# Node logits of a graph layer: from TensorE matmuls to VectorE row sums, with a first stage ordered by hand

## The chip, the core and the metric

The kernel runs on one core of a Trainium2 chip. The metric is device time in microseconds (us) of one execution. Times in the profile count from the first instruction of the profiled execution.

Five engines matter. TensorE (PE in the profile, its weight loads PEld) does matmuls and transposes. VectorE (DVE) and ScalarE (ACT) do element-wise work and reductions. GpSimd (POOL) does some more of these. SyncE (SP) issues transfers. ScalarE and GpSimd issue transfers too; `SPq`, `ACTq` and `POOLq` are their instruction queues.

## What is computed

The reference is two graph layers over N = 4096 nodes with 512 features. Each layer normalises its rows, applies relu, and adds an attention output to its input. All is fp32. The change touches the beginning of layer 0:

```python
h = jnp.maximum(_layernorm(x, axis=-1), 0.0)

# layer 0, with h as its input x
node_att = softmax(x @ node_w, axis=0)          # one logit per node
h = x @ edge_w
e = where(adj > 0, h @ h.T, NEG_BIG)
edge_att = softmax(e, axis=1)
support = x @ weight
output = adj * (node_att * edge_att) @ support + bias
```

So from the normalised rows three products are wanted: `x @ edge_w` (512 columns, kept transposed), `x @ weight` (512 columns, called support), and `x @ node_w` (one column, the node logits).

## The kernel before

The program has five stages, one after the other: (1) the three products above, (2) the scores e with row maxima, written to device memory, (3) the attention of layer 0, (4) the projections of layer 1, (5) the attention of layer 1. Stages 3 and 5 are written in an order by hand, inside `tc.manual_schedule()`: there each engine runs its instructions in the order of the program text. In stages 1, 2 and 4 the framework's scheduler picks the order, by the program's dependencies and its own estimates of time. In both cases the framework adds the waits that the data and the buffers ask for. A pool's `bufs` says how many buffers a tile name rotates through; a new tile waits until the last user of its buffer's former content is done. When a pool closes, its memory goes to pools opened later, and their first tiles wait in the same way.

Stage 1 goes over 32 tiles of 128 rows, four tiles to a block of 512 rows, eight blocks. For each tile:

- SP loads the tile `xt` (L119, 256 KB; four buffers).
- `relu_layernorm` (L65 to L77) computes mean and variance on VectorE (L68, L70), the square root on ScalarE (L72), scale and shift on VectorE (L74, L76), and the normalised row with relu on ScalarE (L77, tile `h`, two buffers).
- TensorE transposes four 128 by 128 pieces of `h` into a PSUM bank `pt` (L124), and VectorE copies them into the block's `h_t` (L125).

For each block of four tiles:

- `edge_w` times the transposed block: four column groups `d`, each four calls of 512 columns summed in a bank `pe` (L129), and copied by ScalarE into `he_t` (L131).
- For each tile, `h_t` times `weight`: four calls of 512 columns summed in a bank `ps` (L136), and copied by VectorE into `sup` (L141). Then four calls with one column each give the tile's logits, in column t of the PSUM tile `lg` (L139).

`pt`, `pe` and `ps` have two PSUM banks each; `lg` has one bank of its own. The weights `we` and `ws` (1024 KB each) and `nw` (the 512 node weights as 128 partitions by 4) come on ScalarE's queue in the order `we`, `ws`, `nw`, after the bias (L93, 256 KB).

At the end of stage 1 the logits go through a softmax over all nodes (L145 to L156): maximum on VectorE, across partitions on GpSimd, exp on ScalarE (L151, with its own table load), sum across partitions on GpSimd (L153), reciprocal and multiplication on VectorE (L155, L156).

Stage 2 (L167 to L216) takes `he_t` against itself. SP loads adjacency tiles `ar` and `ac` (L177, L194), TensorE fills a bank `pe`, one of six (L180, four calls per bank, 512 columns or fewer at the diagonal), ScalarE copies the bank to `es` (L183), and VectorE masks it and takes maxima (L186, L187, and L196 to L201).

Of the kernel before, what the change touches and what calls it, by code (L numbers as in the profile page):

```python
# [8 lines left out]
FP = mybir.dt.float32  # L9
AF = mybir.ActivationFunctionType  # L10
ALU = mybir.AluOpType
AX = mybir.AxisListType
PSUM = bass.MemoryType.PSUM
DRAM = bass.MemoryType.DRAM

P = 128
# [12 lines left out]
def kernel(  # L29
# [15 lines left out]
    nc = tc.nc  # L45
    N, F = x.shape
    H, D = 8, 64
    HG = 4
    NT = N // P
    KC = F // P  # L50
    BL = 512
    NB = N // BL
    TB = BL // P
# [3 lines left out]
    ident = const.tile([P, P], FP, name="ident")  # L57
    make_identity(nc, ident)
    eps = const.tile([P, 1], FP, name="eps")
# [5 lines left out]
    def relu_layernorm(h, xt, pool):  # L65

        st = pool.tile([P, 6], FP, name="st")
        nc.vector.bn_stats(st, xt)  # L68
        mv = pool.tile([P, 2], FP, name="mv")
        nc.vector.bn_aggr(mv, st)  # L70
        sd = pool.tile([P, 1], FP, name="sd")
        nc.scalar.activation(sd, mv[:, 1:2], AF.Sqrt, bias=eps)  # L72
        rs = pool.tile([P, 1], FP, name="rs")
        nc.vector.reciprocal(rs, sd)  # L74
        mr = pool.tile([P, 1], FP, name="mr")
        nc.vector.scalar_tensor_tensor(mr, mv[:, 0:1], -1.0, rs, op0=ALU.mult, op1=ALU.mult)  # L76
        nc.scalar.activation(h, xt, AF.Relu, bias=mr, scale=rs)  # L77
# [12 lines left out]
    sup = big.tile([P, NT, F], FP, name="sup")  # L90
# [8 lines left out]
    he_t = hep.tile([P, KC, N], FP, name="he_t")  # L99

    with tc.tile_pool(name="w0", bufs=1) as wp, tc.tile_pool(name="a0", bufs=2) as ap_, tc.tile_pool(
        name="a0s", bufs=4
    ) as sp, tc.tile_pool(name="a0p", bufs=2, space=PSUM) as pp, tc.tile_pool(
        name="a0l", bufs=1, space=PSUM
    ) as lp:
        we = wp.tile([P, KC, F], FP, name="we")
        ws = wp.tile([P, KC, F], FP, name="ws")
        nw = wp.tile([P, KC], FP, name="nw")
        nc.scalar.dma_start(we, edge_w.rearrange("(k p) f -> p k f", p=P))
        nc.scalar.dma_start(ws, weight.rearrange("(k p) f -> p k f", p=P))  # L110
        nc.scalar.dma_start(nw, node_w)
        lg = lp.tile([P, NT], FP, name="lg")

        for b in range(NB):
            h_t = ap_.tile([P, KC, BL], FP, name="h_t")
            for j in range(TB):
                t = b * TB + j
                xt = sp.tile([P, F], FP, name="xt")
                nc.sync.dma_start(xt, x[t * P:(t + 1) * P, :])  # L119
                h = sp.tile([P, F], FP, name="h", bufs=2)  # L120
                relu_layernorm(h, xt, sp)
                pt = pp.tile([P, KC, P], FP, name="pt")
                for k in range(KC):
                    nc.tensor.transpose(pt[:, k, :], h[:, k * P:(k + 1) * P], ident)  # L124
                nc.vector.tensor_copy(h_t[:, :, j * P:(j + 1) * P], pt)  # L125
            for d in range(KC):
                pe = pp.tile([P, BL], FP, name="pe")
                for k in range(KC):
                    nc.tensor.matmul(pe, we[:, k, d * P:(d + 1) * P], h_t[:, k, :],  # L129
                                     start=(k == 0), stop=(k == KC - 1))  # L130
                nc.scalar.copy(he_t[:, d, b * BL:(b + 1) * BL], pe)  # L131
            for j in range(TB):
                t = b * TB + j
                ps = pp.tile([P, F], FP, name="ps")
                for k in range(KC):
                    nc.tensor.matmul(ps, h_t[:, k, j * P:(j + 1) * P], ws[:, k, :],  # L136
                                     start=(k == 0), stop=(k == KC - 1))
                for k in range(KC):
                    nc.tensor.matmul(lg[:, t:t + 1], h_t[:, k, j * P:(j + 1) * P], nw[:, k:k + 1],  # L139
                                     start=(k == 0), stop=(k == KC - 1))  # L140
                nc.vector.tensor_copy(sup[:, t, :], ps)  # L141


        m1 = sp.tile([P, 1], FP, name="m1")
        nc.vector.tensor_reduce(m1, lg, AX.X, ALU.max)  # L145
        m2 = sp.tile([P, 1], FP, name="m2")
        nc.gpsimd.partition_all_reduce(m2, m1, P, bass_isa.ReduceOp.max)
        m3 = sp.tile([P, 1], FP, name="m3")
        nc.vector.tensor_scalar(m3, m2, -1.0, None, ALU.mult)
        s1 = sp.tile([P, 1], FP, name="s1")  # L150
        nc.scalar.activation(na, lg, AF.Exp, bias=m3, accum_out=s1)  # L151
        s2 = sp.tile([P, 1], FP, name="s2")
        nc.gpsimd.partition_all_reduce(s2, s1, P, bass_isa.ReduceOp.add)  # L153
        s3 = sp.tile([P, 1], FP, name="s3")
        nc.vector.reciprocal(s3, s2)  # L155
        nc.vector.tensor_scalar(na, na, s3, None, ALU.mult)  # L156


    with tc.tile_pool(name="mx", bufs=1) as mxp, tc.tile_pool(name="b_a", bufs=6) as adjp, tc.tile_pool(
        name="b_e", bufs=4  # L160
    ) as esp, tc.tile_pool(name="b_m", bufs=2) as mkp, tc.tile_pool(name="b_s", bufs=2) as sp, tc.tile_pool(
        name="b_p", bufs=6, space=PSUM
# [5 lines left out]
        for i in range(NB):  # L168
            for j in range(i, NB):
                for t in range(i * TB, (i + 1) * TB):  # L170
# [7 lines left out]
                    pe = p_e.tile([P, BL], FP, name="pe")  # L178
                    for k in range(KC):
                        nc.tensor.matmul(pe[:, :w], he_t[:, k, rows], he_t[:, k, cols],  # L180
                                         start=(k == 0), stop=(k == KC - 1))
# [24 lines left out]
            for j in range(TB):  # L206
                t = i * TB + j
# [12 lines left out]
    with tc.tile_pool(name="c_e", bufs=9) as etp, tc.tile_pool(name="c_b", bufs=4) as ebp, tc.tile_pool(  # L220
        name="c_a", bufs=12
    ) as adjp, tc.tile_pool(name="c_w", bufs=3) as wkp, tc.tile_pool(name="c_t", bufs=3) as atp, tc.tile_pool(
        name="c_m", bufs=2
    ) as mxp, tc.tile_pool(name="c_o", bufs=4) as iop, tc.tile_pool(name="c_s", bufs=2) as sp, tc.tile_pool(
        name="c_p", bufs=1, space=PSUM
    ) as p_o, tc.tile_pool(name="c_q", bufs=3, space=PSUM) as p_t, tc.tile_pool(
        name="c_r", bufs=1, space=PSUM
# [34 lines left out]
        def turn(b, m):  # L262

            i = m % TB
            n = TB if m // TB > b else i if m // TB == b else 0
            eb = src[b, m]
            parts = []
            if n > 0:
                pt = p_t.tile([P, BL], FP, name="pt")
                for j in range(n):  # L270
                    nc.tensor.transpose(pt[:, j * P:(j + 1) * P], eb[:, j, i * P:(i + 1) * P], ident)  # L271
                parts.append((slice(0, n * P), pt))
            if n < TB:
                parts.append((slice(n * P, BL), eb[:, i, :] if m // TB == b else eb))
            src[b, m] = parts
# [77 lines left out]
    with tc.tile_pool(name="w1", bufs=1) as wp, tc.tile_pool(name="a1", bufs=3) as sp, tc.tile_pool(  # L353
        name="a1p", bufs=3, space=PSUM
# [15 lines left out]
        for t in range(NT):  # L370
            xt = sp.tile([P, F], FP, name="xt", bufs=4)
            nc.sync.dma_start(xt, x1[t * P:(t + 1) * P, :])
            h = sp.tile([P, F], FP, name="h")
            relu_layernorm(h, xt, sp)
            pt = pp.tile([P, KC, P], FP, name="pt")
            for k in range(KC):
                nc.tensor.transpose(pt[:, k, :], h[:, k * P:(k + 1) * P], ident)
            h_t = sp.tile([P, KC, P], FP, name="h_t")
# [56 lines left out]
    with tc.tile_pool(name="e", bufs=3) as ep, tc.tile_pool(name="e3", bufs=2) as e3p, tc.tile_pool(  # L435
        name="z", bufs=6
    ) as zp, tc.tile_pool(name="rl", bufs=2) as rlp, tc.tile_pool(name="p", bufs=2) as prp, tc.tile_pool(
        name="ac", bufs=2
    ) as acp, tc.tile_pool(name="io1", bufs=2) as iop, tc.tile_pool(name="os", bufs=1) as osp, tc.tile_pool(
        name="s1", bufs=1  # L440
    ) as sp, tc.tile_pool(name="p_v", bufs=1, space=PSUM) as p_v, tc.tile_pool(
        name="p_x", bufs=1, space=PSUM
# [184 lines left out]
```

## Time and profile before

| | us |
|---|---|
| median of 3 runs | 3289.96 (3289.59 to 3289.97) |
| profiled execution | 3290.54 |
| its span, first to last instruction | 3288.7 |
| TensorE busy in the span | 3117.9 (95%) |
| VectorE busy | 2573.5 (78%) |
| ScalarE busy | 1195.6 (36%) |
| GpSimd busy | 1415.7 (43%) |
| last logit matmul of stage 1 starts | about 283.4 |
| first matmul of stage 2 starts | 283.75 |
| last matmul of stage 2 starts | 741.2 |

In the profile a line `L139` is line 139 of the kernel. A group line reads: line, engine, operation, output<-inputs, shapes, count | busy us, mean ns of one | idle time of the engine just ahead of them and what ended it. A chain line reads: start, length in us, what set the time there. A line of busy time by stretch reads: stretch, its length, then busy us and count for TensorE, its weight loads, VectorE, ScalarE and GpSimd, then the granted TensorE clock, the share of DMA, and GB/s. A fp32 matmul call shows as two matmul records, a transpose as one. A matmul's own duration overlaps with its neighbours', so the pace of TensorE is read from starts.

### The profile page before, as it was taken

Reading aid. Unit: us, or ns where it says so; the run is one execution under the profiler, and the core shown is the slowest. Engines: PE = TensorE matmul, PEld = TensorE weight load, DVE = VectorE, ACT = ScalarE, POOL = GpSimd, SP = SyncE. Lnnn points to the kernel's source line nnn. Section 1 sums busy time; section 2 is a strip of 40 time slices with the busy share of each in tenths; the row PEclk is TensorE's granted clock in tenths of the full one; section 3 lists DMA queues with packets and bytes.
Section 4 is the critical chain, followed back from the end, with each engine's and each line's share of the span. In section 5 each row is a group of like instructions: output and inputs, shape, how many; then the busy total and the mean of one; then the engine's idle time right before and its main releaser. Section 6 shows DMA issues by size and latency. Waiting matters only on the chain.

```text
span 3288.7 us, 34545 instructions
## 1 busy us (share of the span) xinstructions
PE 3117.9 (95%) x11514; PEld 1291.8 (39%) x11514; DVE 2573.5 (78%) x3593; ACT 1195.6 (36%) x1417; POOL 1415.7 (43%) x1081
## 2 busy tenths in 40 slices
PE   8999999998999999999998869999999999999997
PEld 4554444444444444444444423232323232323332
DVE  3324777776667678788896599898989898999997
ACT  2211111111111111111113256565656666666664
POOL 0001111113434445445454546565656565655554
PEclk9999999998999999999999989999999999999999
DMA  2104666656444444454433179898988898989896
GB/s 74 39 20 158 225 219 229 223 182 211 142 141 155 142 157 159 141 163 157 147 107 103 36 188 223 228 218 225 219 224 217 222 223 224 222 227 219 227 221 161
DMA packets 239250, 577.07 MB, mean 175 GB/s; under 512 B 26048, under 2 KB 51936, under 8 KB 239072
## 3 DMA queue, kind: packets, MB, share of 16 engines
q1 hardware_dynamic: 163680, 357.76, 32.7%
q0 software_dynamic: 55680, 196.13, 26.9%
q10 hardware_dynamic: 19712, 20.98, 2.1%
q8 instruction: 90, 1.47, 0.2%
q14 instruction: 88, 0.72, 0.1%
HBM read 389.02 MB, written 51.53 MB: 134 GB/s over the span
## 4 chain that ended last, share of the span: by engine, by line
PE 62%; DVE 18%; issue 6%; ACT 6%; DMA 4%; POOL 2%; ACTq 0%; DVEq 0%; SPq 0%; POOLq 0%
PE po L324 26%; PE pe L180 14%; DVE pr L489 13%; PE pv L516 8%; ACT e L474 5%; PE ps L136 3%; PE pe L129 3%; PE dn L522 2%; DMA z<-z_d 2%; PE pd L382 2%; PE pt L271 2%; DMA y<-x 1%; POOL pr L387 1%; PE lg L139 1%; DVE d L283 1%
## 5 line engine op out<-in xcount | busy, mean ns | idle before, releaser
L516 PE MATMUL pv<-pr,va 128*64 128x512 f32 x4096 | 1025.2, 610 | 61.5 <-DVE pr L489 40.2
L324 PE MATMUL po<-sup,at 128*128 128x512 f32 x2048 | 915.2, 598 | 45.1 <-DVE at L291 45.1
L498 POOL TENSOR_TENSOR acc<-acc,pr 128x1024 f32<-128x1024 f32 x240 | 570.3, 2376 | 434.2 <-DVE pr L489 434.0
L489 DVE SCALAR_TENSOR_TENSOR pr<-z,g_m,ex 128x1024 f32<-128x1024 f32 x512 | 631.4, 1273 | 41.9 <-DMA z<-z_d 41.9
L516 PEld LDWEIGHTS pv<-pr,va 128*64 128x64 f32 x4096 | 359.4, 137 | 686.0 <-issue 378.7
L324 PEld LDWEIGHTS po<-sup,at 128*128 128x128 f32 x2048 | 380.2, 192 | 479.7 <-issue 403.7
L301 POOL TENSOR_TENSOR racc<-racc,ex 128x512 f32<-128x512 f32 x240 | 354.7, 1478 | 467.4 <-ACT ex L285 466.8
L285 ACT ACTIVATE ex<-d 128x512 f32<-128x512 f32 x256 | 161.3, 630 | 829.0 <-DVE d L283 829.0
L180 PE MATMUL pe<-he_t 128*128 128x512 f32 (+3 forms) x1152 | 455.8, 557 | 0.1
L465 ACT ACTIVATE ex<-e 128x1024 f32<-128x1024 f32 x256 | 263.1, 1028 | 456.6 <-DVE pr L489 356.9
L486 DVE SCALAR_TENSOR_TENSOR pr<-rl,gd_m,ex 128x1024 f32<-128x1024 f32 x256 | 326.0, 1274 | 29.1 <-ACT ex L465 29.1
L489 DVE SCALAR_TENSOR_TENSOR pr<-z,g_m,e 128x1024 f32<-128x1024 f32 x256 | 327.6, 1280 | 0.0
L477 ACT ACTIVATE rl<-z,ngd_m,d_m 128x1024 f32<-128x1024 f32 x256 | 314.1, 1227 | 26.9 <-DMA z<-z_d 26.9
L180 PEld LDWEIGHTS pe<-he_t 128*128 128x128 f32 x1152 | 212.9, 190 | 234.5 <-issue 222.5
L474 ACT ACTIVATE e<-e,ld_m 128x1024 f32<-128x1024 f32 x256 | 290.0, 1133 | 5.0 <-DMA z_d<-zs 5.0
L283 DVE TENSOR_TENSOR d<-d,mk 128x512 f32<-128x512 f32 x256 | 273.7, 1069 | 8.8
L522 PE MATMUL dn<-pr,d_m 128*32 128x512 f32 x2048 | 273.8, 607 | 0.0
L184 POOL DMA_DIRECT2D e_d<-es x144 | 79.2, 550 | 351.3 <-ACT es L183 345.8
L282 DVE TENSOR_TENSOR d<-pt,mb 128x512 f32<-128x512 f32 (+2 forms) x136 | 87.4, 643 | 172.6 <-PE pt L271 172.6
L183 ACT COPY es<-pe 128x512 f32<-128x512 f32 (+2 forms) x144 | 79.3, 551 | 376.2 <-PE pe L180 376.2
L504 POOL DMA_DIRECT2D acc<-pr x240 | 208.2, 868 | 5.0 <-DVE pr L486 4.0
L291 DVE TENSOR_TENSOR at<-ex,a 128x512 f32<-128x512 f32 x256 | 190.5, 744 | 0.5
(116 smaller groups left out, 2182.9 us busy)
## 6 DMA issues: line engine op xcount, KB each, us to landing
e<-in_adj_t_dram SPq DMA_DIRECT2D x256, 512.0 KB, 4.5
acc<-pr POOLq DMA_DIRECT2D x256, 512.0 KB, 4.9
a<-in_adj_t_dram SPq DMA_DIRECT2D x256, 256.0 KB, 3.4
ar<-in_adj_dram SPq DMA_DIRECT2D x120, 256.0 KB, 3.1
e_d<-es POOLq DMA_DIRECT2D x120, 256.0 KB, 2.8
ac<-in_adj_t_dram SPq DMA_DIRECT2D x112, 256.0 KB, 3.2
eb<-e_d SPq DMA_DIRECT2D x28, 1024.0 KB, 5.8
et<-e_d SPq DMA_DIRECT2D x112, 256.0 KB, 3.5
```

The lines of the kernel that those rows point to most:

```text
L180: nc.tensor.matmul(pe[:, :w], he_t[:, k, rows], he_t[:, k, cols], start=(k == 0), stop=(k == KC - 1))
L283: nc.vector.tensor_tensor(d, d, mk, ALU.add)
L301: nc.gpsimd.tensor_tensor(racc, racc, e, ALU.add)
L324: nc.tensor.matmul(po[j], w[:, j * P:(j + 1) * P], sup[:, m, :], start=(m == 0), stop=last)
L465: nc.scalar.activation(x_, ra.pop((i, m)), AF.Exp)
L474: nc.scalar.activation(x_, ra[i, m], AF.Exp, bias=ld_m[:, h + 3, m:m + 1])
L477: nc.scalar.activation(r, zs_[i, 0], AF.Relu, bias=ngd_m[:, h, m:m + 1], scale=d_m[:, h, m:m + 1])
L486: nc.vector.scalar_tensor_tensor(w, rl.pop((i, m)), gd_m[:, h, m:m + 1], x_, op0=ALU.add, op1=ALU.mult)
L489: nc.vector.scalar_tensor_tensor(w, zs_[i, k], g_m[:, h + k, m:m + 1], e3.pop((i, m)) if k == 3 else x_, op0=ALU.max, op1=ALU.mult)
L498: nc.gpsimd.tensor_tensor(acc[i, 3], acc[i, 3], w, ALU.add)
L516: nc.tensor.matmul(v[c][q][r * D:(r + 1) * D, :], va[:, m, g * HG + k, :], pr[i, m, k][:, q * BL:(q + 1) * BL], **flags)
L522: nc.tensor.matmul(dn[r * Q:(r + 1) * Q, :], d.to_broadcast([P, Q]), pr[i, m, k][:, q * BL:(q + 1) * BL], **flags)
```

## The change

Five things change, all in stage 1.

- The logits are no longer matmuls. For each tile VectorE multiplies `h` by the node weights and sums along the row, in one `tensor_tensor_reduce`, into column t of `lg`, which is now an SBUF tile.
- For that, each partition needs all 512 node weights. `nw` is spread by four small matmuls: column k, repeated 128 times, against the identity puts weights 128k to 128k+127 into every row of `pw`. One VectorE copy takes them to `nw_b`.
- `nw` is loaded first on SP's queue; on ScalarE's queue `ws` now comes ahead of `we`, two transfers as before.
- The stage is in an order by hand. Tiles 0 to 3 are normed one by one, with the support of a tile after the transposes of the next. From then on, a block's four groups of edge products alternate with the transposes of the next block's four tiles, while the tile three ahead is normed; the next block's four supports follow.
- `xt` and the small tiles have eight buffers, `h` five.

The softmax at the end is as it was, inside the order by hand, and stage 2 is unchanged.

```diff
-        name="a0s", bufs=4
-    ) as sp, tc.tile_pool(name="a0p", bufs=2, space=PSUM) as pp, tc.tile_pool(
-        name="a0l", bufs=1, space=PSUM
-    ) as lp:
+        name="a0s", bufs=8
+    ) as sp, tc.tile_pool(name="a0p", bufs=2, space=PSUM) as pp, tc.manual_schedule():
...
+        nw_b = wp.tile([P, F], FP, name="nw_b")
         nw = wp.tile([P, KC], FP, name="nw")
+        nc.sync.dma_start(nw, node_w)
+        nc.scalar.dma_start(ws, weight.rearrange("(k p) f -> p k f", p=P))
         nc.scalar.dma_start(we, edge_w.rearrange("(k p) f -> p k f", p=P))
-        nc.scalar.dma_start(ws, weight.rearrange("(k p) f -> p k f", p=P))
-        nc.scalar.dma_start(nw, node_w)
-        lg = lp.tile([P, NT], FP, name="lg")
-
+
+        pw = pp.tile([P, KC, P], FP, name="pt")
+        for k in range(KC):
+            nc.tensor.matmul(pw[:, k, :], nw[:, k:k + 1].to_broadcast([P, P]), ident, start=True, stop=True)
+        nc.vector.tensor_copy(nw_b.rearrange("p (k q) -> p k q", k=KC), pw)
+        lg = wp.tile([P, NT], FP, name="lg")
+        xts, mvs, sds, hs, hts = {}, {}, {}, {}, {}
+
+        def fetch(t):
+            xts[t] = sp.tile([P, F], FP, name="xt")
+            nc.sync.dma_start(xts[t], x[t * P:(t + 1) * P, :])
+
+        def stats(t):
+            st = sp.tile([P, 6], FP, name="st")
+            nc.vector.bn_stats(st, xts[t])
+            mvs[t] = sp.tile([P, 2], FP, name="mv")
+            nc.vector.bn_aggr(mvs[t], st)
+            sds[t] = sp.tile([P, 1], FP, name="sd")
+            nc.scalar.activation(sds[t], mvs[t][:, 1:2], AF.Sqrt, bias=eps)
+
+        def norm(t):
+            rs = sp.tile([P, 1], FP, name="rs")
+            nc.vector.reciprocal(rs, sds.pop(t))
+            mr = sp.tile([P, 1], FP, name="mr")
+            nc.vector.scalar_tensor_tensor(mr, mvs.pop(t)[:, 0:1], -1.0, rs, op0=ALU.mult, op1=ALU.mult)
+            hs[t] = sp.tile([P, F], FP, name="h", bufs=5)
+            nc.scalar.activation(hs[t], xts.pop(t), AF.Relu, bias=mr, scale=rs)
+
+        def turn(t):
+            b, j = divmod(t, TB)
+            if j == 0:
+                hts[b] = ap_.tile([P, KC, BL], FP, name="h_t")
+            h = hs.pop(t)
+            pt = pp.tile([P, KC, P], FP, name="pt")
+            for k in range(KC):
+                nc.tensor.transpose(pt[:, k, :], h[:, k * P:(k + 1) * P], ident)
+            hw = sp.tile([P, F], FP, name="hw", bufs=2)
+            nc.vector.tensor_tensor_reduce(hw, h, nw_b, 1.0, 0.0, ALU.mult, ALU.add, lg[:, t:t + 1])
+            nc.vector.tensor_copy(hts[b][:, :, j * P:(j + 1) * P], pt)
+
+        def support(t):
+            b, j = divmod(t, TB)
+            ps = pp.tile([P, F], FP, name="ps")
+            for k in range(KC):
+                nc.tensor.matmul(ps, hts[b][:, k, j * P:(j + 1) * P], ws[:, k, :],
+                                 start=(k == 0), stop=(k == KC - 1))
+            nc.vector.tensor_copy(sup[:, t, :], ps)
+
+        def edges(b, d):
+            pe = pp.tile([P, BL], FP, name="pe")
+            for k in range(KC):
+                nc.tensor.matmul(pe, we[:, k, d * P:(d + 1) * P], hts[b][:, k, :],
+                                 start=(k == 0), stop=(k == KC - 1))
+            nc.scalar.copy(he_t[:, d, b * BL:(b + 1) * BL], pe)
+
+        done = {fetch: 0, stats: 0, norm: 0}
+
+        def upto(f, t):
+            while done[f] < min(t + 1, NT):
+                f(done[f])
+                done[f] += 1
+
+        def step(t):
+            if t < NT:
+                ahead = 0 if t < TB else 3
+                for u in range(t, t + ahead + 1):
+                    upto(fetch, u + 4)
+                    upto(stats, u)
+                    upto(norm, u)
+                    upto(stats, u + 1)
+                turn(t)
+
+        for t in range(TB):
+            step(t)
+            if t > 0:
+                support(t - 1)
+        support(TB - 1)
         for b in range(NB):
-            h_t = ap_.tile([P, KC, BL], FP, name="h_t")
             for j in range(TB):
...
+                edges(b, j)
+                step((b + 1) * TB + j)
+            if b + 1 < NB:
+                for j in range(TB):
+                    support((b + 1) * TB + j)
```

What is left out of the diff is the body of the former loop, removed: L117 to L141 as printed above.

More of the change, by code (lines that the diff above doesn't have):

```diff
@@ L114 @@
+        support(TB - 1)
         for b in range(NB):
-            h_t = ap_.tile([P, KC, BL], FP, name="h_t")
             for j in range(TB):
[L117 to L141, printed above, removed]
+                edges(b, j)
```

## The prediction

> **What bounds the kernel now.** I read the page's chain of waits first. It gives TensorE 62% of the span and names three lines of the first stage:
>
> ```profile
> PE 62%; DVE 18%; issue 6%; ACT 6%; DMA 4%; POOL 2%; ACTq 0%; DVEq 0%; SPq 0%; POOLq 0%
> PE po L324 26%; PE pe L180 14%; DVE pr L489 13%; PE pv L516 8%; ACT e L474 5%; PE ps L136 3%; PE pe L129 3%; PE dn L522 2%; DMA z<-z_d 2%; PE pd L382 2%; PE pt L271 2%; DMA y<-x 1%; POOL pr L387 1%; PE lg L139 1%; DVE d L283 1%
> ```
>
> Then I read the same chain in order of time over one block of four tiles (start, length, what), here from 66.18 to 85.92 us:
>
> ```profile
> 66.18 1.72 PE ps L136 x4
> 67.89 0.79 PE lg L139 x8
> 68.68 3.54 PE ps L136 x8
> 72.22 0.79 PE lg L139 x8
> ...
> 80.87 0.79 PE lg L139 x8
> 81.66 0.51 PE pt L124 x4
> 82.25 0.82 ACT h L77
> 83.11 0.66 PE pt L124 x4
> ...
> 85.92 13.92 PE pe L129 x32
> ```
>
> The same piece repeats every 33.67 us (the `ACT h` pieces start at 48.58, 82.25, 115.91, ...). Everything in it is TensorE's, but for one wait for h. Logits (L139) stand on the path, 0.79 us a tile. The last one of the stage is at 282.88, and the second stage's L180 starts at 283.75.
>
> Third, busy time by stretch (TensorE, its loads, VectorE, ScalarE, GpSimd, then clock and DMA): one stretch in the first stage and one in the second.
>
> ```profile
> 100.00:150.00 50.00, 49.41 (x180) 26.74 (x178) 12.47 (x29) 7.34 (x14) 0.00 (x0) 1.00 0.07 21
> 300.00:400.00 100.00, 100.00 (x250) 46.01 (x249) 75.06 (x184) 17.10 (x31) 17.50 (x32) 1.00 0.72 245
> ```
>
> VectorE has 75% free in the first, so it can take work over. The second is TensorE's too: L180 holds the chain without a gap from 283.75 to 741. A start of stage two that is earlier by x ends it earlier by x.
>
> Last, the groups, for durations:
>
> ```profile
> L139 PE MATMUL lg<-nw,h_t 128*128 128x1 f32 x256 | 30.3, 240 | 0.0
> L187 DVE CUSTOM_DVE_ANT_0 mk<-pe,mk 128x512 f32<-128x512 f32 x14 | 9.7, 690 | 9.2 <-ACT es L183 9.0 <-DVE mk L186 0.2
> L187 DVE DVE_READ_ACCUMULATOR2_ANT rm<- 128x1 f32 x17 | 1.4, 83 | 0.0
> ```
>
> L139 has 256 records for 128 calls, two for each fp32 product, as L129 and L136 have. L187 is the same VectorE call that the change uses for row sums.
>
> [...]
>
> **The steady block.** 32 of the 64 wide matmuls take 13.84 us (L129 starts at 52.18, the next line at 66.02), so one takes 0.4287 us with 0.12 for the switch. A group of four transposes takes 0.43 to 0.51.
> - Removed: four logits of 0.81 us (67.73 to 68.54 by start times) = 3.24 us, and the 0.52 us wait for h at 83.1.
> - What is left is 33.67 - 3.76 = 29.91. From below: 64 x 0.4287 + 4 x 0.48 + 0.3 for switches = 29.7. I take 29.8.
> - VectorE per tile: statistics 0.69 + 0.18, scale and shift 0.15 + 0.15, row sum 0.69 + 0.08, two copies 1.38: 3.3 us of a tile's 7.45. ScalarE: 0.29 + 0.81 + 0.58 = 1.7. Both lie beside TensorE.
> - Lead of three: in `step(t)` tile t+3 is normed and t is turned. h(t+3) is queued on ScalarE behind the copy of `edges(b, j)`, so it comes about 1.6 us after that matmul group ends (0.2 + 0.58 + 0.81), and is wanted three steps (3 x 3.9 us) later. `pt`, `pe` and `ps` have two banks each, and each copy is due a step after it can run. So I cost waits in the steady blocks at nothing; the cover is some 10 us, and without it a step pays the 1.6.
> - SP's fetches have eight buffers: x(t+4) goes into one freed four tiles before; DMA is 7% busy here.
>
> **The start.** Here the lead is nought, and VectorE's order puts the copy of `support(t-1)` ahead of the scale of tile t+1.
> - `nw` now goes first on SP. Its issue took 0.88 us on ScalarE's queue, so x slips from 6.2 to about 7.1. The eight small matmuls (about 1.1, as eight transposes took 1.07) and the copy to `nw_b` (0.69) stand ahead of all VectorE work. If `nw` lands by 5 (bias, asked for at 0.72, took 5.7 with 256 KB), `nw_b` is ready at 7.2. If x0 and `nw_b` are ready at 6.4, or `nw_b` only at 9.2, all moves by -0.8 or +2.
> - Statistics from 7.2, h(0) at 9.7, `turn(0)`; then row sum, copy, scale, h(1) at 12.4, `turn(1)`; `support(0)` from 12.95. `ws` is now the first of the two weights, and the first landed at 11.0 (L109); `we` is wanted only at 31.9. So the order of transfers costs nothing.
> - `support(0)` ends at 16.4. Then 0.2 + 0.69 (copy) + 0.3 (scale, shift) + 0.81 (h) = 2.05 us with TensorE idle, before `turn(2)`; the same before `turn(3)`. Four supports of 3.43, two turns of 0.5 and two gaps: 31.9.
> - `edges(0,0)` to 35.3, then 1.6 us idle for h(4), behind its ScalarE copy; `turn(4)` from 36.9. Tiles 4 to 7 are normed in that step in one row, some 1.75 us each, with the row sum and copy of tile 4 behind them on VectorE (43.6). The first that needs its bank is `turn(6)`, at 44.75: 1.1 us to spare. Three more edges, four turns, four supports: 62.9.
>
> **The sum.** 62.9 + 6 blocks x 29.8 + the last four edges 13.7 = 255.4 us, where L180 can start; before it was 283.7. The gain is 28.3 us. Against before, logits give 32 x 0.81 = 25.9 and the waits for h some 4; the start gives back about 2.
>
> **Into the second stage.** Its first adjacency load is issued at 287.46, just after the last softmax step at 287.15 (L156), 3.7 us after TensorE changed over. After, maximum and sum over `lg` run while the last edges do, but the exp is queued on ScalarE behind the last `he_t` copy: 0.8 + 1.28 + 0.29 + 0.19, then GpSimd 0.39 and VectorE 0.16 + 0.24 with hand-overs, again about 3.7. TensorE fills six `pe` buffers meanwhile: (512+384+256+128)/512 + 2 = 4.5 groups of 3.43 = 15.4 us. The first came free at 293.26 (end of L198), 9.6 after the change. So 5.8 us of further delay is hidden; beyond that every us counts.
>
> The profiled execution has 3290.54 us for a span of 3288.7; 3262.2 after the sum. The median shown is 3289.96, hence 3261.7.
>
> **Rivals.**
> 1. *The lead covers only part* (chance 0.14). Say every second block boundary or turn pays: 14 of 28 steps x 1.0 us = 14, to about 3276 (3268 to 3284). Also under this: the second stage, planned by itself, comes out in a worse order and spoils its gapless 457 us. For it: the memset of L167 ran among the softmax steps, so the two stages had been ordered together. Against it: VectorE is at 75% there and TensorE needs no luck.
> 2. *The gain is swallowed* (0.02): loads of the second stage start late enough to stop TensorE. That takes 5.8 + 28.3 = 34 us of delay, and 3290 results. Nothing in the page is that late.
> 3. *Slower* (0.04): the order by hand makes TensorE wait at every step, because the lead isn't real (tile t's h is tied to the copy just before it). Then each of the 28 steps costs the startup's 1.6 to 2.05 us: 45 to 57, less 28.3: 3307 to 3319. It decides from 28.3 / 28 = 1.0 us a step on. Against it: h has five buffers, four of them live.
> That the row sum isn't off TensorE can't be: no matmul writes `lg` any more.
>
> **How the numbers follow.** My forecast, with 0.80, is 3256 to 3268: start +2 or -0.8, a block 0.3 lower to 0.7 higher over six (-2 to +4). A floor is 235.5 us of pure TensorE work (512 x 0.4287 + 32 x 0.5) from 9.7 on, 245, thus 3252. To hold 8 in 10 with part of rival 1, the range is 3255 to 3271. About 0.2% (6.6 us) is what a measurement of this kernel can tell from no change. Forecast and rival 1 lie below it: 0.94 faster; 0.02 within; 0.04 slower.
>
> **What would show it.** L180's first matmul at 255 (252 to 264). Blocks 29.8 us apart. Two idle gaps of 2 us for h ahead of the third and fourth group of transposes, one of 1.6 ahead of the fifth, and none later. Row sums of 690 + 83 ns, 32 of each. First adjacency load 3 to 5 us after L180 starts, and no wait at L180. Wrong, if TensorE waits for h or for a copy past 50 us, or if the span from L180's start to the end isn't 3005 us within 3.

## The result

The changed kernel takes 3261.2 us, median of 4 runs (3256.1 to 3263.1), against 3289.8 us for the kernel before in the same rounds. The ratio is 0.9915, with a 95% interval of 0.9897 to 0.9932: 0.85% faster. The forecast was 3261.7 us. The profiled execution has 3259.88 us and a span of 3258.1. Lines have moved: L180 of before, the first matmul of stage 2, is now L235; the edge products are L162, the supports L155, the transposes L146, h L137, the row sum L148.

The page's chain of waits, after. The logits are gone from it; the edge products and supports are still there with 3% each:

```profile
PE 61%; DVE 19%; issue 6%; ACT 6%; DMA 4%; POOL 2%; ACTq 0%; DVEq 0%; POOLq 0%; SPq 0%
PE po L379 26%; PE pe L235 14%; DVE pr L544 14%; PE pv L571 8%; ACT e L529 5%; PE pe L162 3%; PE ps L155 3%; DMA z<-z_d 2%; PE dn L577 2%; PE pd L437 2%; PE pt L326 2%; POOL pr L442 1%; DMA y<-x 1%; ACT ex L520 1%; DVE d L338 1%
```

The same chain in order of time (start, length, what), one block and the end of the stage:

```profile
95.52 3.43 PE pe L162 x8
98.95 0.44 PE pt L146 x4
99.39 3.43 PE pe L162 x8
...
110.57 0.44 PE pt L146 x4
111.00 13.74 PE ps L155 x32
124.74 3.43 PE pe L162 x8
...
241.63 13.75 PE pe L162 x32
255.38 0.02 issue
255.40 0.59 ACT he_t L164
...
256.04 44.09 PE pe L235 x114
```

A block now takes 124.74 - 95.52 = 29.22 us; it took 33.67. Nothing in it belongs to another engine. At the end there is a wait that was nearly hidden before: stage 2's first matmul starts 0.66 us after the last edge products, behind ScalarE's copy of them.

TensorE's instructions in order of time at the start of the stage (start, length, line, shapes, idle before and what ended it):

```profile
10.87 1.12 PE L146 MATMUL pt<-ident,h 128*128 128x128 f32 x4 [3.16 <-ACT h L137]
13.88 1.11 PE L146 MATMUL pt<-ident,h 128*128 128x128 f32 x4 [1.89 <-ACT h L137]
14.79 5.27 PE L155 MATMUL ps<-ws,h_t 128*128 128x512 f32 x8
21.95 0.66 PE L146 MATMUL pt<-ident,h 128*128 128x128 f32 x4 [1.89 <-ACT h L137]
...
27.94 0.66 PE L146 MATMUL pt<-ident,h 128*128 128x128 f32 x4 [1.89 <-ACT h L137]
...
35.30 3.60 PE L162 MATMUL pe<-h_t,we 128*128 128x512 f32 x8
40.28 0.66 PE L146 MATMUL pt<-ident,h 128*128 128x128 f32 x4 [1.39 <-ACT h L137]
```

The three idle gaps ahead of the third, fourth and fifth group of transposes are the forecast ones. A full group of eight wide matmuls reads 3.60 here, as its last end is modelled; by the pace, 3.43 a group, the gaps are 0.17 us longer than the brackets say. The first support (14.79) reads 5.27, and that was not forecast.

The groups of the first stage and its busy time in one stretch (TensorE, loads, VectorE, ScalarE, GpSimd, clock, DMA share, GB/s):

```profile
L148 DVE CUSTOM_DVE_ANT_0 hw<-h,nw_b 128x512 f32<-128x512 f32 x32 | 21.3, 665 | 0.2
L148 DVE DVE_READ_ACCUMULATOR2_ANT lg<- 128x1 f32 x32 | 2.6, 83 | 0.0
```

```profile
100.00:150.00 50.00, 50.00 (x139) 23.50 (x138) 20.85 (x56) 10.83 (x23) 0.00 (x0) 1.00 0.15 43
```

The row sums cost VectorE 24 us in all (665 + 83 ns each; 690 + 83 were forecast), and it still has more than half of the stretch free; TensorE has none.

Stage 2 now starts at 256.04 in place of 283.75, which is 27.7 us earlier. Its matmuls take 457.5 us as before (457.4). The rest of the profiled gain is in the stages behind that, and no part of the change: from the start of stage 2 to the end of the span it is 3004.9 us before and 3002.1 after, while the twelve profiled executions of this study have 2997.7 to 3007.4 there with the same code. So the measure below is where stage 2 starts; the time is given beside it.

### The profile page after: what moved, and what is told of

It is laid out like the page before. It is cut to its first block, busy times and chain, and to the rows that moved or that the text cites. A ratio compares the mean times of both kernels' runs of the same rounds, so it can differ in the third digit from the quotient of the medians.

```text
span 3258.1 us, 34087 instructions
## 1 busy us (share of the span) xinstructions
PE 3092.7 (95%) x11266; PEld 1265.4 (39%) x11266; DVE 2598.7 (80%) x3658; ACT 1193.0 (37%) x1417; POOL 1415.1 (43%) x1081
## 4 chain that ended last, share of the span: by engine, by line
PE 61%; DVE 19%; issue 6%; ACT 6%; DMA 4%; POOL 2%; ACTq 0%; DVEq 0%; POOLq 0%; SPq 0%
PE po L379 26%; PE pe L235 14%; DVE pr L544 14%; PE pv L571 8%; ACT e L529 5%; PE pe L162 3%; PE ps L155 3%; DMA z<-z_d 2%; PE dn L577 2%; PE pd L437 2%; PE pt L326 2%; POOL pr L442 1%; DMA y<-x 1%; ACT ex L520 1%; DVE d L338 1%
## 5 line engine op out<-in xcount | busy, mean ns | idle before, releaser
L235 PE MATMUL pe<-he_t 128*128 128x512 f32 (+3 forms) x1152 | 455.8, 557 | 0.7 <-ACT he_t L164 0.7
L235 PEld LDWEIGHTS pe<-he_t 128*128 128x128 f32 x1152 | 212.9, 190 | 235.8 <-issue 222.5
## 6 DMA issues: line engine op xcount, KB each, us to landing
a<-in_adj_t_dram SPq DMA_DIRECT2D x256, 256.0 KB, 3.1
ar<-in_adj_dram SPq DMA_DIRECT2D x120, 256.0 KB, 2.9
e_d<-es POOLq DMA_DIRECT2D x120, 256.0 KB, 2.7
ac<-in_adj_t_dram SPq DMA_DIRECT2D x112, 256.0 KB, 3.1
et<-e_d SPq DMA_DIRECT2D x112, 256.0 KB, 3.2
```

## The experiments

Each kernel was profiled once, the changed kernel twice. Its two profiles differ by 1.4 us in where stage 2 starts, all of it from the start of stage 1; so a difference of that size between two kernels means nothing by itself. Each ratio is to runs of the kernel before in the same rounds, so it differs a little from the quotient of the medians shown.

The theory: the removed logit matmuls are nearly the whole gain, since they stood on the path that sets the end, and the order by hand adds little because its start gives back what its steady part wins. The first rival: the order is the gain. The second: the lead of three tiles is what keeps the order from being slower than before.

| kernel | stage 2 starts (us) | median (us) | ratio to before (95%) |
|---|---|---|---|
| before | 283.75 | 3289.8 | |
| changed | 256.0 | 3261.2 | 0.9915 (0.9897 to 0.9932) |
| order alone | 281.6 | 3288.3 | 0.9994 (0.9987 to 1.0) |
| row sums alone | 257.7 | 3262.9 | 0.9912 (0.9896 to 0.9929) |
| lead 0 | 298.8 | 3304.0 | 1.0038 (1.0023 to 1.0053) |
| lead 1 | 258.1 | 3260.1 | 0.9907 (0.9892 to 0.9921) |
| start with lead 1 | 249.6 | 3255.1 | 0.9895 (0.9879 to 0.9912) |
| start: lead, pace, later copy | 247.7 | 3253.0 | 0.9885 (0.9872 to 0.9899) |
| changed, again | 257.5 | 3261.6 | 0.9914 (0.99 to 0.9927) |

**The order alone.** The logits go back to TensorE:

```diff
-            nc.vector.tensor_tensor_reduce(hw, h, nw_b, 1.0, 0.0, ALU.mult, ALU.add, lg[:, t:t + 1])
...
+            for k in range(KC):
+                nc.tensor.matmul(lg[:, t:t + 1], hts[b][:, k, j * P:(j + 1) * P], nw[:, k:k + 1],
+                                 start=(k == 0), stop=(k == KC - 1))
             nc.vector.tensor_copy(sup[:, t, :], ps)
```

> The order by hand with the logits as matmuls again (four one-column calls behind each tile's support, lg in PSUM; no spreading of the node weights, no row sums). Theory (the removed logit matmuls are nearly the whole gain, and the order itself wins only the waits for h, less what its start gives back): the first stage ends at 256.0 + 32 x 0.81 = 281.9 us, 281 to 283 with a start that no longer waits for the spread weights; the time is 3286 to 3290. Rival (the order is the gain, and the row sums only ride on it): the stage ends before 272, the time is below 3280.

Measured: stage 2 starts at 281.6, 2.1 us earlier than before. In time that can't be told from nothing: 0.9994, with 1.0 at the edge of the interval. The rival wanted less than 272. The chain of this run over one block:

```profile
70.31 3.54 PE pe L159 x8
...
89.34 0.79 PE lg L152 x8
90.12 3.54 PE ps L149 x8
93.67 0.78 PE lg L152 x8
...
103.11 3.54 PE pe L159 x8
```

A block takes 32.80 us, 0.87 less than before and 3.58 more than in the changed kernel. From one group of logits to the next it is 4.33 us (89.34 to 93.67), and eight support matmuls alone take 3.43. So a tile's logits cost 0.90 us here, and not the 0.81 from their own start to the next: the support behind them takes 3.54.

**The row sums alone.** The kernel before, its order by the scheduler kept:

```diff
+        pw = pp.tile([P, KC, P], FP, name="pt")
+        for k in range(KC):
+            nc.tensor.matmul(pw[:, k, :], nw[:, k:k + 1].to_broadcast([P, P]), ident, start=True, stop=True)
+        nc.vector.tensor_copy(nw_b.rearrange("p (k q) -> p k q", k=KC), pw)
...
                 nc.vector.tensor_copy(h_t[:, :, j * P:(j + 1) * P], pt)
+                nc.vector.tensor_tensor_reduce(hw, h, nw_b, 1.0, 0.0, ALU.mult, ALU.add, lg[:, t:t + 1])
...
-                for k in range(KC):
-                    nc.tensor.matmul(lg[:, t:t + 1], h_t[:, k, j * P:(j + 1) * P], nw[:, k:k + 1],
-                                     start=(k == 0), stop=(k == KC - 1))
```

> The kernel before with the row sums alone: order by the scheduler as before, four xt buffers, the node weights first on SP and spread by the four small matmuls, we before ws. Theory: 283.75 - 32 x 0.81 = 257.8 us for the first stage; the waits for h of the old order stay, and a row sum of 0.77 us may stand ahead of a copy of transposed pieces once or twice per block, which adds nothing to 12: 258 to 270, the likeliest 260, the time 3263 to 3276. Rival (the order is the gain): the stage ends after 275, the time is above 3280.

Measured: 257.7, which is 26.05 us earlier than before, against 32 x 0.81 = 25.9. The time is the changed kernel's within its scatter. The chain of this run still has the wait for h once in each block; its last three lines are the change of stage:

```profile
47.28 0.82 ACT h L77
48.10 0.13 issue
48.23 0.63 PE pt L127 x4
...
65.61 11.16 PE ps L141 x26
...
77.29 0.82 ACT h L77
...
256.86 0.69 DVE sup L143
257.55 0.15 DVE acc L169
257.70 12.30 PE pe L182 x40
```

So its block takes 30.01 us (77.29 less 47.28), 3.66 less than before: four times the 0.90 that a tile's logits cost in the order by hand, too. That 26.05 is so near to 25.9 is therefore partly luck. From the first edge products to stage 2 it is 236.0 us here (from 21.70) and 264.3 before (from 19.47), 28.3 less; of that the later start takes 2.2. In the chain of the start an x tile lands at 12.76 (10.77 before), and the copy of the node weights and two row sums follow; what made the tile late was not tested.

The order by hand takes 0.8 us out of each block, 5.5 over seven, yet ends only 1.7 us earlier (0.2 by the second profile of the changed kernel). The wait at the change of stage is no longer there than in this run, so its start gives the rest back, some 4 us. In the steady blocks no row sum came in ahead of a needed copy in a way that shows, so that part of the expectation was too cautious; in the start two did, and TensorE waited 0.36 us for the copy behind them. Alone, the two parts give 2.1 + 26.05 = 28.2 us, together 27.7: within the scatter of the start they add up. The first rival is out.

**A lead of nought and of one.**

```diff
-                ahead = 0 if t < TB else 3
+                ahead = 0
```

```diff
-                ahead = 0 if t < TB else 3
+                ahead = 0 if t < TB else 1
```

> The changed kernel with a lead of nought everywhere: each tile is normed in the step that turns it. Theory: each of the 28 steps of the steady part pays what the first one paid in the changed kernel, 1.54 us (hand-over, copy of he_t on ScalarE, h): 27 more x 1.54 = 42, the first stage ends at 298, the time is 3303. Rival (the lead does nothing, since ScalarE is mostly idle): 256 and 3261.

> The changed kernel with a lead of one tile in place of three. Theory: h of the next tile is ready some 1.6 us after a group of edge products ends and is wanted 3.9 us after that, so a lead of one hides it all: the first stage ends at 256 (within 0.5), the time is that of the changed kernel. Rival (three are needed, since ScalarE's and VectorE's queues couple the tiles): the stage ends after 265.

With a lead of nought, every step of the steady part has the gap (TensorE in order of time):

```profile
75.27 0.66 PE L146 MATMUL pt<-ident,h 128*128 128x128 f32 x4 [1.39 <-ACT h L137]
75.77 3.60 PE L162 MATMUL pe<-h_t,we 128*128 128x512 f32 x8
80.75 0.66 PE L146 MATMUL pt<-ident,h 128*128 128x128 f32 x4 [1.39 <-ACT h L137]
```

A step takes 80.75 - 75.27 = 5.48 us in place of 3.87, so 1.61 more. Stage 2 starts at 298.8, and the kernel is slower than before, 3304.0 us: the prediction's third rival, with its mechanism and nearly its price (it said 3307 to 3319). With a lead of one the gap is gone. Stage 2 starts at 258.1, outside the 0.5 that was expected, but from the first edge products on (37.38 against 35.30) the two are alike: 220.7 us to the start of stage 2 in both. The 2.1 us are the start's, where the second support ran slow as well. So one tile of lead hides what three hide.

**The start with a lead of one.** This is for the gaps, and for a version that beats the changed kernel:

```diff
-                ahead = 0 if t < TB else 3
+                ahead = 1 if t < TB else 3
```

> The changed kernel with a lead of one tile in the start too (tiles 0 to 3), three afterwards as before. Theory (the three idle gaps of the start come from the scale of a tile being queued on VectorE behind the copy of a support, and from h(4) being queued on ScalarE behind a copy of he_t): both gaps of 2.05 us and the one of 1.54 go, the first stage ends 5.6 us earlier, at 250.4, or 248 to 253 with the scatter of the first landings; the time is about 3255. Rival (the gaps are x tiles that come late): they stay, 256.

Measured: 249.6 and 3255.1. After the first support TensorE has no gap up to stage 2, so all three came from the queues and none from late x tiles.

**The slow first support.** In the changed kernel the eight matmuls of the first support take some 5.1 us, not 3.43; the first four start 0.85 us apart, the others 0.43. Two causes were at hand: transfers into the same memory, which go on until about 17 us, or TensorE itself after a pause. This run fills pauses with matmuls that nobody reads:

```diff
+        dm = pp.tile([P, BL], FP, name="pe")
+
+        def warm(n):
+            for _ in range(n):
+                nc.tensor.matmul(dm[:, :P], ident, ident, start=True, stop=True)
+
+        warm(8)
         pw = pp.tile([P, KC, P], FP, name="pt")
...
+        warm(6)
         for t in range(TB):
             step(t)
+            if t == 0:
+                warm(6)
```

> The changed kernel with idle TensorE time at the start filled: 8 + 6 + 6 matmuls of the identity with itself into a bank that nobody reads, before and after the matmuls that spread the node weights and after the first transposes. Theory (TensorE runs at half pace after having been idle, and that stretched the first support from 3.43 to 5.1 us and the spreading to 2.04): the first support takes 3.4 to 3.9 us, the first stage ends 1 to 2.5 us earlier. Rival (the first support is slow because transfers of x and the weights write into the same memory until about 18 us): it still takes about 5, from the same start.

TensorE in order of time, this run; L162 is here the support:

```profile
14.10 3.60 PE L162 MATMUL ps<-ws,h_t 128*128 128x512 f32 x8
19.60 0.66 PE L153 MATMUL pt<-ident,h 128*128 128x128 f32 x4 [1.90 <-ACT h L144]
20.09 5.29 PE L162 MATMUL ps<-ws,h_t 128*128 128x512 f32 x8
```

The first support is at full pace, at about the same time (14.10 against 14.79) and under no fewer transfers: in the four us from 14 DMA moved 387, 381, 238 and 98 GB/s in this run, and 387, 383, 207 and 121 in the changed kernel. So transfers are not the cause. But the stage ended later (stage 2 from 257.1): the half pace came back in the second support, and again in the third, each behind a gap of 1.9 us. The granted clock of the second says so too. Busy time over the second support of this run (the seventh figure is the granted clock, the eighth the share of DMA):

```profile
20.10:24.00 3.90, 3.90 (x8) 1.71 (x7) 0.87 (x3) 0.00 (x0) 0.00 (x0) 0.60 0.22 67
```

Transfers had fallen to 22% by then. So the half pace goes with TensorE's pauses, though not every pause brings it: in the changed kernel the second support follows a gap of 1.89 us and runs at full pace. That filling some pauses gains time by itself was wrong, as long as others follow. (One run, 3264.1 us.)

**All of it together.** Lead of one in the start, the pauses filled, and the copy of the node weights moved from its old place to behind the scale of tile 0 (the other edits are those above, with five matmuls in place of six after the first transposes):

```diff
                     upto(norm, u)
+                    if t == 0 and u == 0:
+                        nc.vector.tensor_copy(nw_b.rearrange("p (k q) -> p k q", k=KC), pw)
```

> The changed kernel with three edits of the start together: a lead of one tile for tiles 0 to 3 (ended the first stage at 249.6 alone), matmuls of the identity with itself in TensorE's idle time there (8 + 6 + 5), and the copy of the spread node weights behind the scale of tile 0 on VectorE. Theory: with no idle gap left after the first support, the pace won there stays won: 249.6 - 1.7 (first support at full pace) - 0.7 (copy of the weights beside h) = 247.2 for the end of the first stage (245 to 250), the time about 3253, some 8 us below the changed kernel. Rival (half pace only moves to a later group, as it did when the gaps were there): 249 to 250, no better than the lead alone.

> The changed kernel itself, as the measure for the run beside it: first stage to end at 255 to 258, time 3258 to 3264.

TensorE in order of time, the run with all of it; L161 is the support:

```profile
13.87 3.70 PE L161 MATMUL ps<-ws,h_t 128*128 128x512 f32 x8 [0.50 <-DVE h_t L155]
17.41 0.60 PE L152 MATMUL pt<-ident,h 128*128 128x128 f32 x4
17.85 3.60 PE L161 MATMUL ps<-ws,h_t 128*128 128x512 f32 x8
```

Full pace from the first support on, and it stays, though DMA moved 385, 383 and 324 GB/s in the three us from 14. Stage 2 starts at 247.7, 1.8 us earlier than with the lead alone. Nearly all of this is the pace: the first support takes 3.54 us to the next start here and 5.17 there (14.07 to 19.24), while it starts only 0.2 earlier. Of the 0.7 expected of the later copy, no more than that 0.2 shows. The time is 3253.0 us (3248.5 to 3253.6), against 3261.6 (3257.8 to 3267.2) for the changed kernel on the same chip: 8.6 us less, and the two sets of runs don't overlap. This is the fastest version here.

**The order of the two weights.**

```diff
-        nc.scalar.dma_start(ws, weight.rearrange("(k p) f -> p k f", p=P))
         nc.scalar.dma_start(we, edge_w.rearrange("(k p) f -> p k f", p=P))
+        nc.scalar.dma_start(ws, weight.rearrange("(k p) f -> p k f", p=P))
```

> The changed kernel with edge_w ahead of weight, as before. Theory (the order of the two transfers matters only if weight lands after the first support could start, at 14.8 us): now weight is issued only when the bias has landed, at 6.7, and takes about 10 us, so the first support starts at 16.5 to 17 in place of 14.8, and the first stage ends about 2 us later, near 258. Rival (it costs nothing, as the prediction had the order): the first support starts at 14.8.

```profile
16.17 5.69 PE L155 MATMUL ps<-ws,h_t 128*128 128x512 f32 x8 [1.74 <-DMA ws<-in_weight_dram]
```

Measured as the theory had it: TensorE waits 1.74 us for `ws`, and stage 2 starts at 257.8. With supports ahead of edge products in the start, `ws` first is worth about that: the second support starts at 24.25 here, and at 22.45 and 22.17 in the two profiles of the changed kernel, of which the second lost 1.7 us to a slow third support later. (One run, 3265.4 us; by time alone it can't be told from the changed kernel.)

**The wait at the change of stage.** The last block's supports go behind its edge products:

```diff
-            if b + 1 < NB:
+            if b + 2 < NB:
                 for j in range(TB):
                     support((b + 1) * TB + j)
+        for j in range(TB):
+            support((NB - 1) * TB + j)
```

> The changed kernel with the last block's four supports after its edge products, so that the stage ends on a VectorE copy out of a ps bank and not on ScalarE's copy to he_t. It tells apart what the second stage's first matmul waits for (0.66 us in the changed kernel). If it is he_t as a whole: the wait goes, as he_t is finished 14 us before. If it is the stage's PSUM banks (the last copy out of any): it waits about as long, now for VectorE's copy to sup. The adjacency loads start about 1 us after the change-over in place of 2.8, since the exp need not wait for the last he_t copy; that changes no time. First stage to end within 1 us of 256, the scatter of the start apart.

VectorE's and TensorE's instructions there (L237 is stage 2's first matmul):

```profile
256.39 0.69 DVE L157 COPY sup<-ps 128x512 f32<-128x512 f32 x1 [2.74 <-PE ps L155]
```

```profile
257.23 4.96 PE L237 MATMUL pe<-he_t 128*128 128x512 f32 x12 [0.88 <-DVE m L202]
```

The wait stays, 0.88 us, and L237 starts 0.15 us after the copy out of the last `ps` bank ends, although it reads nothing of `sup`. So it is not `he_t` as a whole. It fits the reuse of PSUM banks from stage to stage. The run with the row sums alone has it too: there the last copy of `sup` ends at 257.55 and stage 2 starts at 257.70. So has the trace of before: the copy ended at 283.61 and L180 starts at 283.75, some 0.2 us later than behind a group of logits elsewhere; most of the copy ran under the last logits. The profile names VectorE's next instruction (L202) as the releaser here. But in the trace of before L180 starts while that instruction still runs:

```profile
283.70 0.19 DVE L145 TENSOR_REDUCE m<-lg 128x1 f32<-128x32 f32 x1
```

So the wait is taken to end with the copy. That it is for the banks is argued, not tested. The expected early exp was a miss: the softmax's first step stands behind the last `sup` copy on VectorE, and the first adjacency load came 2.2 us after the change-over. Stage 2 started at 257.2. (One run, 3263.6 us.)

## Why the prediction was right

The time (3261.7 against 3261.2) and the start of stage 2 (255.4 against 256.0) are closer than the steps they were built from, and that closeness is luck. Point by point:

- **The logits.** Right in mechanism: they stood on TensorE's path, and taking them off gave their time back. In size, 25.9 us were forecast and 26.05 measured apart, but two errors met there. A tile's logits cost 0.90 us and not 0.81 (28.8 for 32), and the run with the row sums alone starts 2.2 us later and waits some 0.6 longer at the change of stage, which leaves about 26.
- **The steady block.** 29.8 forecast, 29.22 measured, six times: 3.5 us too much. From above, 3.76 were taken off, where 4.45 went: 3.6 for the logits, and 0.8 to 0.9 for the order, where the wait for h was put at 0.52. Even the bound from below, 29.7, was too high. It took 0.48 us for four transposes, where they take 0.44, and 0.3 for switches, where there are none: 64 x 0.4287 + 4 x 0.44 = 29.2.
- **The start.** First edge products forecast at 31.9, measured at 35.3: 3.4 us too little. Of these, 1.2 were there at the first transposes (10.87 against 9.7): the node weights landed at 5.5 and their spreading took 2.04 us, not 1.1. Another 0.3 came until the second group (VectorE waited 0.54 us for x1), and 0.4 in that group, which was slow (0.91 us to the next start, 0.50 later). Some 1.7 are the first support at half pace. The trace of before showed such slow work at its start (the lines below this list); the prediction took the pace of the steady part. The gaps, 2.06, 2.06 and 1.56 us by the pace, were as forecast (2.05, 2.05 and 1.6). That forecast takes it that what is queued behind a waiting copy waits too. The trace of the changed kernel shows it: the input of tile 2's scale was there at 14.12, VectorE was idle for 4.38 us up to 20.09, and the scale ran at 20.70, behind the copy of the first support.
- **Into stage 2.** "No wait at L180" was wrong by 0.66 us, a term that it put at nothing: the stage now ends on a copy out of a bank that no TensorE work covers. The first adjacency load comes 2.8 us after L235 starts (3.7 forecast, with 3 to 5 as the sign); the table load ahead of the exp takes 1.28 of it (from 256.01; as long in the trace of before, from 284.68). TensorE doesn't wait for that first load of adjacency, as forecast.
- **What the order gives.** Forecast: some 4 us from the waits for h, about 2 given back. Measured against the row sums alone: 5.5 won in the blocks, some 4 given back by the start, 1.7 net in one profile and 0.2 in the other.
- **The rest.** 3005 us within 3 was forecast; 3002.1 was measured. The bound of 3 was too narrow: three of the twelve executions had 2997.7 to 3000.1.
- **The rivals.** The lead covers everything (first rival out), nothing is swallowed (second out). The third is a true mechanism that this kernel avoids: without a lead it is slower than before.

Eight transposes at the start and eight in a steady block, in the trace of before:

```profile
12.93 1.94 PE L124 MATMUL pt<-ident,h 128*128 128x128 f32 x8 [12.93 <-ACT h L77]
47.85 1.07 PE L124 MATMUL pt<-ident,h 128*128 128x128 f32 x8
```

So the errors of the start (+3.4), the blocks (-3.5) and the change-over (+0.66) nearly cancel. The logits carry the result.

## What to carry to other kernels

Ask of a small matmul not how much it computes but whether it stands on TensorE's path: here four calls of one column cost 0.90 us a tile, and the steady part got that back in full when another engine with free time took them over, in either order of the rest. Price such a group by the distance between its neighbours with and without it, not by its own length. An order by hand needs a lead wherever a tile's preparation is queued behind a copy that waits for TensorE (a step took 5.48 us without one here, 3.87 with), and one tile is enough when the preparation (1.6 us) is shorter than a step (3.9 us); look for the same pattern in the start, where it was left out. When a forecast is met, check its terms apart, since two of them here were wrong by 3.5 us in opposite directions.

## What was unexpected of the hardware

TensorE ran at half pace after pauses (wide fp32 matmuls 0.85 us apart, not 0.43). Where the half pace came back later in a run, the granted clock in the profile shows it (0.60, above). Over the first support of the changed kernel it reads 1.00, though the matmuls stand just as far apart:

```profile
14.80:18.20 3.40, 3.40 (x6) 1.34 (x6) 0.69 (x1) 0.00 (x0) 0.00 (x0) 1.00 0.64 236
```

The trace's record of the clock begins only at 18.14 us in this run (at 17.09 in the trace of before), about where full pace sets in, and what has no record counts as 1.00 in that column. So at the start of a program the pace has to be read from the starts of the matmuls.

How long the half pace lasted differs. In the run with the pauses filled the second support reads 5.29 us, and the third and fourth 8.69, where 3.60 and 7.03 are full pace. So each time 1.7 us were lost, which is four matmuls at half pace, some 3.4 us. At the start of that run it lasted longer: the first matmuls, back to back from 1.56 to 6.94 (24 records in 5.38 us, where 12 take 1.50 later), were all slow. And the half pace returned behind gaps of 1.9 us, in some executions and not in others. In the second profile of the changed kernel the third support was slow as well, and stage 2 started at 257.5 and not 256.0:

```profile
28.16 8.73 PE L155 MATMUL ps<-ws,h_t 128*128 128x512 f32 x16
```

These are two supports, which take 7.03 in the first profile. So a gap of 2 us can cost 3.7, with the 1.7 of the slow support behind it, and part of the scatter of the start comes from it.

A transfer of 2 KB, the first on its queue, took 2.8 to 4.8 us from issue to landing at the start of the program, over eleven profiled executions.
